# Layer norm of the first half's tokens: normalized and turned on VectorE in the second half's key stage, kept turned in DRAM, and read back for the feed-forward

## The chip, the cores and the metric

The kernel runs on one core of one Trainium2 chip. The metric is the device time of one execution in microseconds (us). The times of the kernel before are the median of three runs and one profiled execution, from which every trace line here is taken.

## What is computed

A gated cross-attention block with a feed-forward layer, on 32 sequences of 64 tokens with 512 features, all in float32. The reference, cut to what matters:

```python
x = x + tanh(g_xattn[0]) * xattn(layernorm(x), ctx, mask, bias, Wq, Wk, Wv, Wo)   # 32 heads of 128
x = x + tanh(g_ffn[0]) * ffn(layernorm(x), weight, bias, lora_A, lora_B, starts)

def ffn(x, ...):                     # x: 32 x 64 x 512
    y = einsum('bsd,od->bso', x, weight) + bias
    lo = einsum('bsr,bor->bso', einsum('bsd,brd->bsr', x, A), Bw)   # rank 16, adapter by sequence
    return y + where(use_lora, lo, 0)
```

The change concerns the second layer norm: the tokens that come out of the attention are normalized along their 512 features, and must then stand with the features along the partitions, so that TensorE can multiply them with `weight`.

## The kernel before, in words

The 2048 tokens are worked on in two halves (`p` = 0 and 1), of 1024 tokens each: `NT` = 8 tiles of 128 tokens, or `NCH` = 2 chunks of 512. Each half goes through a key stage (16 units, one for each pair of heads), a value stage (4 groups of 4 units) and the attention proper (queries, scores, softmax, values, output projection). The feed-forward layer for all four chunks comes at the very end, after the attention of the second half. Every float32 matrix is split into a high and a low float32r part, and a product is three matmuls (`mm3`, line 93, its matmul is line 98). The key, value and query products use a scheme of seven block products for eight (`unit`, line 354): px (p1, later p2 on top), py (p6), pv (p7, later p4 on top) and pz (p5, later p3 on top), each in a bank of PSUM (8 banks in all). VectorE adds a product to the destination (line 356), and only then may the later product be accumulated in the same bank. The last two products of a unit (p4 and p3, `end`, line 381) and the store of its keys to DRAM (`kd`, line 720) are carried into the next unit, after its first product.

The order of the instructions on each engine is written out by hand. Side work is written as generators in a list, `streams`, and `beat()` (line 64) advances each of them by one step after each product; `drain()` runs one to its end. What an engine is given is executed in that order; it waits for its operands where they come from another engine or from a DMA. All DMAs but two of the first are issued by SP, in the order in which they are written, and SP waits for the source or the buffer of each.

In the key stage (`stage_a`, line 684) GpSimd prepares the next unit's key weights (`key_blocks`, line 592; its `fetch`, line 259, loads `rawk`), VectorE computes the moments of `x` (`x_stats`, line 620, through the two-buffer pool `rows`, tag `row`, line 54), and later the weights of the first value group (`blocks_v`). Key tiles (`kT`) live in a pool of two buffers. After the key stage, `x_norm` (line 644) normalizes the transposed `x` with rows of means and scales that it loads from DRAM (`ln`, from `lnd`, line 641).

The output of the first half's attention, `acc`, is stored to DRAM as `x1d` (line 1048). Its moments are computed by `acc_stats` (line 674) in the second half's key stage, from unit 3 on, and its scales by `acc_rstd` (line 679), 28 small VectorE operations that join `streams` in the second value group (line 735).

At the end, `oproj2` (line 1035) does the last eight steps of the output projection (12 matmuls each) and calls `beside(t)` (line 1340) after each. For chunk 0, `beside` normalizes a tile (`ffn_norm`, line 1224, from `x1t`, which `x1_load`, line 1175, has loaded back from `x1d`) into `xn`, and two steps later `ffn_tile` (line 1228) turns it by four TensorE transposes (line 137) into a PSUM bank, from which ScalarE makes the high part (line 1234) and VectorE the low part (line 1235) of the feed-forward's operand `fa`. `ffn_chunk(c)` (line 1273) multiplies chunk c: first the low-rank part (`ffn_lora`, 8 matmuls), then four token tiles (`ffn_out`, 14 matmuls each). Between them it normalizes and turns the tiles of chunk c + 1. Chunks 0 and 1 are the first half's tokens, chunks 2 and 3 those of the second half, which never leave SBUF.

Of the kernel before, what the change touches and what calls it, by code (L numbers as in the profile page):

```python
# [9 lines left out]
F32 = mybir.dt.float32  # L10
F32R = mybir.dt.float32r
# [6 lines left out]
P = 128  # L18
D = 512
KT = D // P  # L20
# [23 lines left out]
def flamingo_block(ctx: ExitStack, tc: tile.TileContext, x, xT, ctxT, bias, mask, gx, gf,  # L44
# [30 lines left out]
    ident = const.tile([P, P], F32, name="ident")  # L75
    make_identity(nc, ident)
    x1d = dram.tile([NT * P, D], F32, name="x1d")
    kd = [[dram.tile([P, 2, TP], F32, name=f"kd{p}_{n}") for n in range(NPR)] for p in range(NPH)]
    lnd = [dram.tile([2, NT, P], F32, name=f"lnd{p}") for p in range(NPH)]
    vd = [[dram.tile([P, NT, 512], F32, name=f"vd{p}_{g}") for g in range(2 * NG)] for p in range(NPH)]  # L80
# [331 lines left out]
    def k_tile(g):  # L412
        return kqp.tile([P, 2, TP], F32, tag="kq", name=f"kT{g}")
# [172 lines left out]
    def paced(g, k):  # L586
        for _ in g:
            yield
            for _ in range(k - 1):
                yield  # L590
# [43 lines left out]
    def x_spread(p):  # L634
        mv, y = mvx[p], rx[p]
        m, mt = [st.tile([P, 4, NT], F32, tag=f"m{i}", name=f"m{i}{p}", bufs=1) for i in range(2)]
        for i in range(4):
            nc.vector.tensor_copy(m[:, i], y if i % 2 else mv[:, :, 0])
        nc.vector.transpose(mt.rearrange("p a b -> p (a b)"), m.rearrange("p a b -> p (a b)"))
        for i in range(4):  # L640
            nc.sync.dma_start(out=lnd[p].rearrange("s t (b q) -> b (s t) q", b=4)[i],
                              in_=mt[i * 32:i * 32 + 2 * NT].rearrange("p a b -> p (a b)"))
# [36 lines left out]
    def acc_rstd(p):  # L679
        for c in range(p * NCH, (p + 1) * NCH):  # L680
            yield from ln_rstd(mv2[:, c * 4:(c + 1) * 4, :], f"f{c}", rstd, c, 5)
            yield

    def stage_a(p, first, fc, res, rot, more, enter, blocks):
        xc, plain = first
        f = None
        for n in range(NPR):
            g = p * NPR + n
            if n == 0 and plain:
                sums = sum_blocks(fc, res, f"c{p}", nc.vector, xc)  # L690
                streams.append(sums)
            if n == 0 and not plain:
                drain(blocks)
            if n == (1 if plain else 0):
                streams.append(key_blocks(p, n + 1))
            if n == 3:
                f = [big(f"f{j}", [P, KT, 512], F32, f"xf{p}_{j}") for j in range(2)]
                t7 = big(rot[7], [P, 2, 1024], F32, f"wvr{p}_0a")
                t8 = big(rot[8], [P, 2, 1024], F32, f"wvr{p}_0b")
                fetch_v(p, 0, [t7[:, 0], t7[:, 1], t8[:, 0], t8[:, 1]])  # L700
                if more:
                    streams.append(paced(more, 2))
                xstat = x_stats(p)
                streams.append(xstat)
            if n == 5:
                vsum = [None] + [rwp.tile([P, 1024], F32, tag=f"r{2 + i}", name=f"vs{p}_0_{i}") for i in range(2)] + [None]
                v0 = paced(blocks_v(p, 0, rot, vsum, nc.vector, K_ORDER), 3)
                streams.append(v0)
            if 6 <= n < 6 + KT:
                for j in range(NCH):  # L710
                    nc.sync.dma_start(out=f[j][:, n - 6, :], in_=xT[p * NCH + j, n - 6])
            if n == 10:
                drain(xstat)
                x_spread(p)
            kt = k_tile(g)
            w = wt[("k", g)]

            def store(kt=kt, n=n):
                for i in range(2):
                    nc.sync.dma_start(out=kd[p][n][:, i, :], in_=kt[:, i, :])  # L720
            if n < 2 and plain:
                for j in range(2):
                    plain_half(w, plain, k_dst(kt), f"k{g}", j, plain["ps"] if n == 0 and j == 0 else None)
                store()
            else:
                if n == 2 and plain:
                    drain(sums)
                carry[:] = [unit(w, xc, None, k_dst(kt), f"k{g}", tuple(carry)), store]
        drain(v0)
        xnorm = paced(x_norm(p, f), 2)  # L730
        streams.append(xnorm)
        xq = {}
        for g in range(NG):
            if g == 1 and p:
                streams.append(acc_rstd(p - 1))
            if g == 2:
                drain(xnorm)
                streams.append(mask_stream(p))
                if p == 0:
                    streams.append(adapt)  # L740
            if g == NG - 1:
                t4 = pieces(rwp.tile([P, 1024], F32, tag="r1", name=f"x{p}t4"))
                fetch("q", p * NPR, "r0")
                bias = enter()
                streams.append(turned_blocks(f, [rot[(7 * NG + i) % 9] for i in range(7)], f"x{p}", nc.gpsimd, keep,
                                             t4, xq, bias, enter))
            for t in range(4):
                if t == 1:
                    if g + 1 < NG:
                        raw = [rwp.tile([P, 1024], F32, tag=f"r{i}", name=f"wvr{p}_{g + 1}_{i}") for i in range(4)]  # L750
                        fetch_v(p, g + 1, raw)
                        streams.append(blocks_v(p, g + 1, rot, None, nc.gpsimd, V_ORDER))
                    if g == NG - 2:
                        keep = {}
                        streams.append(turned_sums(f, f"x{p}", nc.gpsimd, keep))
                if t == 2 and g == NG - 1:
                    streams.append(prep("q", p * NPR, nc.gpsimd))
                vt = kqp.tile([P, 4, 512], F32, tag="kq", name=f"vt{p}_{g}_{t}")
                dst = {(i, j): vt[:, i * 2 + j, :] for i in range(2) for j in range(2)}
                after = unit(wt["v", p, g], xc, slice(t * P, (t + 1) * P), dst, f"v{p}_{g}_{t}", tuple(carry))  # L760

                def store(vt=vt, g=g, t=t):
                    for i in range(2):
                        for j in range(2):
                            nc.sync.dma_start(out=vd[p][2 * g + i][:, j * 4 + t, :], in_=vt[:, i * 2 + j, :])
                carry[:] = [after, store]
        enter()
        return xq
# [434 lines left out]
    def ffn_weights(tags):  # L1203
        wf = [big(tags[i], [P, KT, 512], F32R, f"wf{i}") for i in range(2)]
        ffn_w.update(wf=wf, tags=tags)
        ffn_w["xn"] = big(tags[6], [P, 4, D], F32, "xn")
        ar, br, a2 = ffn_w["ar"], ffn_w["br"], ffn_w["a2"]

        b2 = ffn_w["b2"] = [wbp.tile([P, 512], F32R, tag="wb", name=f"b2{i}") for i in range(2)]
        for _ in range(8):  # L1210
            yield
        nc.scalar.copy(b2[0], br)
        nc.scalar.copy(b2[1][64:P, :], br[64:P, :])
        nc.gpsimd.tensor_tensor(b2[1][0:64, :], br[0:64, :], b2[0][0:64, :].bitcast(F32), ALU.subtract)
        yield
        nc.scalar.copy(a2[:, :, 0:NL * R], ar)
        nc.gpsimd.tensor_tensor(a2[:, :, 64:64 + NL * R], ar, a2[:, :, 0:NL * R].bitcast(F32), ALU.subtract)
        yield
        for kt in range(KT):
            split(ffn_w["raw"][:, kt, :], wf[0][:, kt, :], wf[1][:, kt, :], nc.gpsimd)  # L1220
            yield
        streams.append(paced(x1_load(1), 2))
# [5 lines left out]
    def ffn_tile(c, t):  # L1228
        if t == 0:
            act[c] = [big(ffn_w["tags"][2 + 2 * (c % 2) + i], [P, KT, 512], F32R, f"fa{c}_{i}") for i in range(2)]  # L1230
        hi, lo = act[c]
        ps = transposes(ffn_w["xn"][:, t, :], f"f{c}_{t}")
        h = hi[:, :, t * P:(t + 1) * P]
        nc.scalar.copy(h, ps)
        nc.vector.tensor_tensor(lo[:, :, t * P:(t + 1) * P], ps, h.bitcast(F32), ALU.subtract)

    def ffn_lora(c):
        hi, lo = act[c]
# [34 lines left out]
    def ffn_chunk(c, beside=lambda t: None):  # L1273
        more = c + 1 < NPH * NCH
        ffn_lora(c)
        for t in range(4):
            if more:
                ffn_tile(c + 1, t)
                if t < 3:
                    ffn_norm(c + 1, t + 1)  # L1280
            ffn_out(c, t)
            beside(t)
# [4 lines left out]
    for p in range(NPH):  # L1287
# [34 lines left out]
        else:  # L1322
# [16 lines left out]

            def beside(t):  # L1340
                if t < 4:
                    ffn_norm(0, t)
                else:
                    moments(t - 4)
                if 1 < t < 6:
                    ffn_tile(0, t - 2)
                elif t == 6:
                    ffn_norm(1, 0)

            def rest_of(t):  # L1350
                if t == 0:
# [59 lines left out]
```

## Time and profile before

| | |
|---|---|
| median of 3 runs | 1527.27 us (1527.03 to 1527.68) |
| profiled execution, its own time | 1527.01 us |
| its span, first to last instruction | 1525.2 us |
| TensorE (PE) busy | 1518.5 us, 100% of the span |
| VectorE (DVE), ScalarE (ACT), GpSimd (POOL) busy | 62%, 47%, 69% |
| granted TensorE clock | 1.000 |
| second half's key stage, value stage | about 732 to 881 us, 881 to 1033 us |
| last eight projection steps and feed-forward | about 1433 to 1522 us |

A row of a group of instructions names the line, the engine, the operation, the tile written and the tiles read, the shapes and the number of instructions; after the first bar the busy time and the mean of one in ns, after the second the idle time of the engine just before them and what ended most of it. A row in order of time begins with the start and the length in us, and ends with the idle time before it in brackets. PEld is TensorE's weight load, SPq the queue of DMAs that SP issues. A row on DMA packets gives their number and bytes, and the last figure of a row that begins with q1 is the time that these packets took, as a share of the 16 DMA engines in that stretch.

### The profile page before, as it was taken

The page shows a single profiled execution, that of the slowest core. Times are in us where ns is not written, and L with a number is a line of the kernel's source. Part 1 is how long each engine was busy: PE and PEld are TensorE (multiplying, and loading weights), DVE is VectorE, ACT ScalarE, POOL GpSimd, SP SyncE. Part 2 cuts the span into 40 slices and gives each one's busy share as a digit, 9 for nine tenths or more (in the row PEclk, how much of TensorE's full clock was granted, in tenths as well). Part 3 has the DMA queues.
Part 4 walks back from the last instruction along what each step waited for, and adds up shares of the span by engine and source line. Part 5 has one row for each costly group of instructions (what it writes and reads, how often), then busy time and mean ns, then how long its engine had stood idle before and what let it go on. Part 6 is the DMA issues. An engine that isn't in the chain of part 4 may idle for free.

```text
span 1525.2 us, 25056 instructions
## 1 busy us (share of the span) xinstructions
PE 1518.5 (100%) x8984; PEld 1279.1 (84%) x8984; DVE 941.6 (62%) x1575; ACT 718.4 (47%) x1586; POOL 1048.9 (69%) x1160
## 2 busy tenths in 40 slices
PE   9999999999999999999999999999999999999998
PEld 7888888888888888888888888888888888888887
DVE  5675554376676566666386558437667656666663
ACT  5444233355654664466344423335565466546511
POOL 4999378968675657668789847896867566757310
PEclk9999999999999999999999999999999999999999
DMA  5754544384335263532475454438434426353211
GB/s 207 276 194 152 196 170 168 138 303 157 128 139 180 85 233 126 178 116 95 166 261 194 152 200 166 167 139 312 159 117 143 176 97 222 126 186 113 69 42 69
DMA packets 111071, 248.51 MB, mean 163 GB/s; under 512 B 10241, under 2 KB 44033, under 8 KB 106850
## 3 DMA queue, kind: packets, MB, share of 16 engines
q1 hardware_dynamic: 110658, 246.38, 46.0%
q8 instruction: 71, 1.16, 0.3%
q10 hardware_dynamic: 288, 0.52, 0.1%
q14 instruction: 54, 0.44, 0.1%
HBM read 173.45 MB, written 73.42 MB: 162 GB/s over the span
## 4 chain that ended last, share of the span: by engine, by line
PE 98%; DVE 1%; issue 0%; ACT 0%; POOL 0%; DVEq 0%; POOLq 0%; ACTq 0%
PE pa L98 23%; PE po L982 8%; PE pzv L98 6%; PE pvv L98 6%; PE pxv L98 6%; PE pvq L98 6%; PE pzq L98 6%; PE pxq L98 5%; PE pzk L98 5%; PE pvk L98 5%; PE pxk L98 5%; PE ps L838 4%; PE pyv L98 3%; PE pyq L98 3%; PE pyk L98 3%; PE pf L98 2%
## 5 line engine op out<-in xcount | busy, mean ns | idle before, releaser
L98 PE MATMUL pa<-wo,ch 128*128 128x512 f32 x896 | 278.5, 392 | 0.0
L873 ACT COPY pt<-tp 32x256 f32<-32x256 f32 x456 | 184.0, 403 | 61.0 <-DVE tp L876 50.5
L98 PEld LDWEIGHTS pa<-wo,ch 128*128 128x128 f32 x896 | 166.5, 188 | 34.7
L98 PE MATMUL pa<-wo,cl 128*128 128x512 f32 x448 | 174.8, 390 | 0.0
L1031 DVE TENSOR_TENSOR acc<-pa,acc 128x512 f32<-128x512 f32 x192 | 129.2, 681 | 53.5 <-PE pa L98 53.5
L791 POOL TENSOR_TENSOR sm<-sm,madd 128x512 f32<-128x512 f32 x60 | 77.0, 1295 | 87.1 <-DMA sm<-bias 87.1
L865 POOL TENSOR_TENSOR sm<-sm,r 128x512 f32<-128x512 f32 x64 | 66.9, 1045 | 74.4 <-DVE r L864 73.2
L982 PEld LDWEIGHTS po<-pt,v 128*128 128x128 f32 x960 | 111.6, 192 | 2.2
L982 PE MATMUL po<-pt,v 128*128 128x128 f32 x960 | 112.5, 275 | 0.0
L843 POOL TENSOR_TENSOR sm<-sm,mx 128x512 f32<-128x512 f32 x64 | 66.9, 1047 | 59.8 <-DVE mx L842 59.8
L987 DVE TENSOR_TENSOR cl<-po,ch 128x512 fp32r<-128x512 f32 x112 | 76.5, 690 | 46.1 <-ACT ch L986 45.5
L356 DVE TENSOR_TENSOR vt<-pvv,vt 128x512 f32<-128x512 f32 x64 | 44.0, 688 | 92.7 <-PE pvv L98 92.7
L98 PEld LDWEIGHTS pa<-wo,cl 128*128 128x128 f32 x448 | 84.1, 188 | 18.5 <-DVE cl L987 0.9
L90 POOL TENSOR_TENSOR wo<-rawo,wo 128x512 fp32r<-128x512 f32 x60 | 76.1, 1292 | 22.9 <-ACT wo L89 22.9
L356 DVE TENSOR_TENSOR qT<-pvq,qT 128x512 f32<-128x512 f32 x64 | 44.1, 689 | 73.6 <-PE pvq L98 73.6
L986 ACT CAST ch<-po 128x512 fp32r<-128x512 f32 x112 | 65.6, 589 | 50.1 <-PE po L982 48.1
L356 DVE TENSOR_TENSOR kT<-pvk,kT 128x512 f32<-128x512 f32 x60 | 41.3, 688 | 73.1 <-PE pvk L98 72.8
L378 ACT COPY vt<-pxv 128x512 f32<-128x512 f32 x32 | 18.8, 588 | 131.0 <-PE pxv L98 131.0
L852 ACT ACTIVATE sm<-sm 128x512 f32<-128x512 f32 x60 | 38.0, 633 | 79.0 <-POOL sm L843 75.8
L356 DVE TENSOR_TENSOR qT<-pzq,qT 128x512 f32<-128x512 f32 x64 | 44.2, 691 | 38.1 <-PE pzq L98 37.4
L192 POOL TENSOR_TENSOR vs<-wvr,wvr 128x512 f32<-128x512 f32 x24 | 31.2, 1313 | 48.6 <-DMA wvr<-wv 28.7
L838 PEld LDWEIGHTS ps<-kB,qT 128*64 128x64 f32 x2048 | 61.2, 138 | 3.6 <-issue 1.4
(1001 smaller groups left out, 3908.6 us busy)
## 6 DMA issues: line engine op xcount, KB each, us to landing
kd<-kT SPq DMA_DIRECT2D x64, 512.0 KB, 3.9
vd<-vt SPq DMA_DIRECT2D x128, 256.0 KB, 2.3
kB<-kd SPq DMA_DIRECT2D x32, 1024.0 KB, 9.9
v<-vd SPq DMA_DIRECT2D x32, 1024.0 KB, 7.5
rawq<-wq SPq DMA_DIRECT2D x32, 512.0 KB, 3.3
sm<-bias SPq DMA_DIRECT2D x64, 256.0 KB, 4.3
rawo<-wo SPq DMA_DIRECT2D x32, 512.0 KB, 3.5
rawk<-wk SPq DMA_DIRECT2D x31, 512.0 KB, 5.4
```

The costliest lines, as they stand in the source:

```text
L90: eng.tensor_tensor(lo, raw, hi.bitcast(F32), ALU.subtract)
L98: nc.tensor.matmul(ps, a, b, start=start and i == 0, stop=stop and i == 3 * n - 1, skip_group_check=True)
L356: nc.vector.tensor_tensor(o, ps, i, ALU.add)
L791: nc.gpsimd.tensor_tensor(t, t, masks[p][0], ALU.add)
L838: nc.tensor.matmul(ps[h * S:(h + 1) * S, t, :], qT[:, i, tok], kT[:, i, tok], start=True, stop=True)
L843: nc.gpsimd.tensor_tensor(s, s, mx.unsqueeze(2).to_broadcast([P, NT, S]), ALU.subtract)
L865: nc.gpsimd.tensor_tensor(t, t, r.unsqueeze(2).to_broadcast([P, NT, S]), ALU.mult)
L873: f(pts[n == NPR - 2][dst, i, :, src], of[src, :, ki * 32:(ki + 1) * 32])
L982: nc.tensor.matmul(ps[:, t * P:(t + 1) * P], b["v", n][:, c * 4 + t, i * P:(i + 1) * P], pts[n == NPR - 2][:, i, c * 4 + t, :], start=True ...
L986: nc.scalar.copy(h[:, i, sl], ps)
L987: nc.vector.tensor_tensor(lo[:, i, sl], ps, h[:, i, sl].bitcast(F32), ALU.subtract)
L1031: nc.vector.tensor_tensor(acc[t], ps, acc[t], ALU.add)
```

## The change

The first half's tokens no longer wait for the end. In the second half's key stage, once their moments are there (the rest of `acc_stats` is drained in unit 6), `acc_rstd` follows at once. From unit 11 on a new generator, `acc_turned`, takes the eight tiles one after the other: it loads a tile from `x1d` into a `row` buffer, normalizes it in place on VectorE three steps later, turns it on VectorE into a second `row` buffer (`nc.vector.transpose` turns each block of 32 x 32 by itself), and one step later stores it by four DMAs to a new DRAM tensor `xtd` (512 features x 1024 tokens), each of which takes 32 partitions and puts their 16 blocks where they belong: 512 pieces of 128 bytes. One tile takes four steps. It is drained before the value stage goes on.

At the end, `ffn_load(c)` loads a chunk of `xtd` (four DMAs of 128 x 512), and `ffn_given(c, kt)` only splits a quarter of it into the high and the low part. For chunks 0 and 1 this takes the place of `ffn_norm` and `ffn_tile`. Chunks 2 and 3 are as before. Chunk 0 is loaded where `ffn_weights` begins, chunk 1 after the fourth of the last projection steps, into the same buffer.

```diff
--- before.py
+++ after.py
@@ -75,6 +75,7 @@
     ident = const.tile([P, P], F32, name="ident")
     make_identity(nc, ident)
     x1d = dram.tile([NT * P, D], F32, name="x1d")
+    xtd = dram.tile([D, TP], F32, name="xtd")
     kd = [[dram.tile([P, 2, TP], F32, name=f"kd{p}_{n}") for n in range(NPR)] for p in range(NPH)]
     lnd = [dram.tile([2, NT, P], F32, name=f"lnd{p}") for p in range(NPH)]
     vd = [[dram.tile([P, NT, 512], F32, name=f"vd{p}_{g}") for g in range(2 * NG)] for p in range(NPH)]
@@ -681,6 +682,23 @@
             yield from ln_rstd(mv2[:, c * 4:(c + 1) * 4, :], f"f{c}", rstd, c, 5)
             yield
 
+
+    def acc_turned(p):
+        for t in range(NT):
+            c = p * NCH + t // 4
+            xt = rows.tile([P, D], F32, tag="row", name=f"xr{p}_{t}")
+            nc.sync.dma_start(out=xt, in_=x1d[t * P:(t + 1) * P, :])
+            for _ in range(3):
+                yield
+            ln_apply(xt, xt, mv2[:, c * 4:(c + 1) * 4, :], rstd[c], t % 4)
+            tp = rows.tile([P, D], F32, tag="row", name=f"xq{p}_{t}")
+            nc.vector.transpose(tp, xt)
+            yield
+            for i in range(4):
+                nc.sync.dma_start(
+                    out=xtd.rearrange("(a b) t -> b a t", b=32)[:, :, t * P + i * 32:t * P + (i + 1) * 32],
+                    in_=tp[i * 32:(i + 1) * 32].rearrange("p (a b) -> p a b", b=32))
+
     def stage_a(p, first, fc, res, rot, more, enter, blocks):
         xc, plain = first
         f = None
@@ -699,7 +717,8 @@
                 t8 = big(rot[8], [P, 2, 1024], F32, f"wvr{p}_0b")
                 fetch_v(p, 0, [t7[:, 0], t7[:, 1], t8[:, 0], t8[:, 1]])
                 if more:
-                    streams.append(paced(more, 2))
+                    more = paced(more, 2)
+                    streams.append(more)
                 xstat = x_stats(p)
                 streams.append(xstat)
             if n == 5:
@@ -709,9 +728,15 @@
             if 6 <= n < 6 + KT:
                 for j in range(NCH):
                     nc.sync.dma_start(out=f[j][:, n - 6, :], in_=xT[p * NCH + j, n - 6])
+            if n == 6 and p:
+                drain(more)
+                streams.append(acc_rstd(p - 1))
             if n == 10:
                 drain(xstat)
                 x_spread(p)
+            if n == 11 and p:
+                turned_acc = acc_turned(p - 1)
+                streams.append(turned_acc)
             kt = k_tile(g)
             w = wt[("k", g)]
 
@@ -727,12 +752,12 @@
                     drain(sums)
                 carry[:] = [unit(w, xc, None, k_dst(kt), f"k{g}", tuple(carry)), store]
         drain(v0)
+        if p:
+            drain(turned_acc)
         xnorm = paced(x_norm(p, f), 2)
         streams.append(xnorm)
         xq = {}
         for g in range(NG):
-            if g == 1 and p:
-                streams.append(acc_rstd(p - 1))
             if g == 2:
                 drain(xnorm)
                 streams.append(mask_stream(p))
@@ -1203,7 +1228,7 @@
     def ffn_weights(tags):
         wf = [big(tags[i], [P, KT, 512], F32R, f"wf{i}") for i in range(2)]
         ffn_w.update(wf=wf, tags=tags)
-        ffn_w["xn"] = big(tags[6], [P, 4, D], F32, "xn")
+        ffn_load(0)
         ar, br, a2 = ffn_w["ar"], ffn_w["br"], ffn_w["a2"]
 
         b2 = ffn_w["b2"] = [wbp.tile([P, 512], F32R, tag="wb", name=f"b2{i}") for i in range(2)]
@@ -1233,6 +1258,17 @@
         h = hi[:, :, t * P:(t + 1) * P]
         nc.scalar.copy(h, ps)
         nc.vector.tensor_tensor(lo[:, :, t * P:(t + 1) * P], ps, h.bitcast(F32), ALU.subtract)
+
+
+    def ffn_load(c):
+        ffn_w["xt"] = big(ffn_w["tags"][6], [P, KT, 512], F32, f"xt{c}")
+        for kt in range(KT):
+            nc.sync.dma_start(out=ffn_w["xt"][:, kt, :], in_=xtd[kt * P:(kt + 1) * P, c * 512:(c + 1) * 512])
+
+    def ffn_given(c, kt):
+        if kt == 0:
+            act[c] = [big(ffn_w["tags"][2 + 2 * (c % 2) + i], [P, KT, 512], F32R, f"fa{c}_{i}") for i in range(2)]
+        split(ffn_w["xt"][:, kt, :], act[c][0][:, kt, :], act[c][1][:, kt, :], nc.vector)
 
     def ffn_lora(c):
         hi, lo = act[c]
@@ -1274,7 +1310,12 @@
         more = c + 1 < NPH * NCH
         ffn_lora(c)
         for t in range(4):
-            if more:
+            if c + 1 < NCH:
+                for kt in range(KT)[2 * t:2 * t + 2]:
+                    ffn_given(c + 1, kt)
+                if t == 1:
+                    ffn_w["xn"] = big(ffn_w["tags"][6], [P, 4, D], F32, "xn")
+            elif more:
                 ffn_tile(c + 1, t)
                 if t < 3:
                     ffn_norm(c + 1, t + 1)
@@ -1339,13 +1380,11 @@
 
             def beside(t):
                 if t < 4:
-                    ffn_norm(0, t)
+                    ffn_given(0, t)
                 else:
                     moments(t - 4)
-                if 1 < t < 6:
-                    ffn_tile(0, t - 2)
-                elif t == 6:
-                    ffn_norm(1, 0)
+                if t == 3:
+                    ffn_load(1)
 
             def rest_of(t):
                 if t == 0:
```

## The prediction, made before the changed kernel was run

> **What bounds the kernel now.** I read the busy table first, then the chain of work that ended last, then the end of the run in order of time, then the stage into which the work is moved.
>
> ```profile
> PE 1518.5 (100%) x8984; PEld 1279.1 (84%) x8984; DVE 941.6 (62%) x1575; ACT 718.4 (47%) x1586; POOL 1048.9 (69%) x1160
> ...
> PE 98%; DVE 1%; issue 0%; ACT 0%; POOL 0%; DVEq 0%; POOLq 0%; ACTq 0%
> ```
>
> TensorE is the path for 98% of the span. So an instruction taken from TensorE is worth its own length, and anything else costs nothing until it makes TensorE wait. What is removed stands in these rows (groups by line in the last 100 us):
>
> ```profile
> L1235 DVE TENSOR_TENSOR fa<-tpf,fa 128x512 fp32r<-128x512 f32 x16 | 10.9, 682 | 3.0 <-ACT fa L1234 3.0
> ...
> L137 PE MATMUL tpf<-ident,xn 128*128 128x128 f32 x64 | 9.8, 275 | 0.3 <-DVE xn L132 0.2
> ...
> L1234 ACT CAST fa<-tpf 128x512 fp32r<-128x512 f32 x16 | 9.3, 584 | 40.2 <-PE tpf L137 40.2
> ```
>
> Matmuls overlap, so their 275 ns are not their price. The price is read from the rhythm of the projection's last steps, from one accumulation to the next (12 matmuls with, then without, four transposes between):
>
> ```profile
> 1447.53 0.69 DVE L1046 TENSOR_TENSOR acc<-pa,acc 128x512 f32<-128x512 f32 x1 [1.45 <-PE pa L98]
> ...
> 1450.74 0.69 DVE L1046 TENSOR_TENSOR acc<-pa,acc 128x512 f32<-128x512 f32 x1 [1.13 <-PE pa L98]
> ...
> 1456.65 0.69 DVE L1046 TENSOR_TENSOR acc<-pa,acc 128x512 f32<-128x512 f32 x1 [0.78 <-PE pa L98]
> ```
>
> 3.21 us with transposes; the step to 1453.93 still has them, the one to 1456.65 has none and takes 2.72. Four transposes cost 0.48 us. The new work goes into the second half's key stage. There the chain is TensorE alone, 1.36 us for a product of six matmuls, seven products (9.52 us) a unit, and SP issues three large transfers a unit (start, length, queue, line, transfer):
>
> ```profile
> 838.61 0.80 SPq L720 DMA_DIRECT2D kd<-kT  x2
> 839.49 0.74 SPq L264 DMA_DIRECT2D rawk<-wk  x1
> ...
> DMA packets 432, 1.57 MB, mean 183 GB/s; under 512 B 48, under 2 KB 48, under 8 KB 432
> ...
> q1 hardware_dynamic: 432, 1.57, 50.7%
> ```
>
> The last two lines are the DMA view of 839.4 to 848: 1.5 MB of payload keeps 16 engines 50.7% busy for 8.6 us, 4.3 us of ring time in a unit. In 825 to 850 VectorE is 59% busy. It has time, but works in order, and each wait for a DMA holds the PSUM reads behind it.
>
> **What the Trainium skill says.** "DMA: Bandwidth & Descriptors", section "Queues, rings and completion order": one issuing engine has one ring on each DMA engine, consumed in ring order. So a load issued behind stores waits for them. No run here shows it directly. Same page, "Specifications": full rate needs 512 B or more; smaller is read-modify-write. This trace has one store of 128-byte pieces, `lnd` (line 641), four issues in 826 to 829.2:
>
> ```profile
> DMA packets 128, 0.01 MB, mean 3 GB/s; under 512 B 128, under 2 KB 128, under 8 KB 128
> ...
> q1 hardware_dynamic: 128, 0.01, 2.4%
> ...
> DMA packets 1040, 1.05 MB, mean 140 GB/s; under 512 B 16, under 2 KB 1040, under 8 KB 1040
> ...
> q1 hardware_dynamic: 1040, 1.05, 42.8%
> ```
>
> 2.4% of 16 engines for 3.2 us is 1.23 us for 128 packets, 9.6 ns each; half are completions, so data packets lie between 9.6 and 19 ns, in an idle ring. No penalty shows, but nothing was saturated. The last pair (1400 to 1407.5, a `v` load) gives 50 ns at 1 KB; `out` stores give 88 at 2 KB. That line meets 128 B near 17 ns. Same page, "Alternative transpose paths": VectorE turns 32 x 32 blocks only. It agrees with the code, which places the blocks by four DMAs. The 128x512 transpose of line 876 takes 0.695 us in 62 runs.
>
> **The change, part by part.**
>
> *Removed from TensorE.* 32 transposes, eight groups of four. Four sit in the projection's last steps: 4 x 0.48 = 1.92. Four sit in feed-forward chunk 0, which takes 16.86 us (1456.45 to 1473.31); without transposes a chunk is 8 x 0.227 + 4 x 3.17 = 14.50, so 2.36, small waits for `xn` included. **Gain 4.28 us, all on the path.**
>
> *Added in the tail.* Eight splits from SBUF (ScalarE copy, VectorE subtract) replace eight from PSUM and eight `xn` (0.54 us): no more work. `xt0` is four loads issued near 1408, behind `v`; its first use is after 1437. `xt1` is issued near 1447 and used at 1459; a 256 KB `x1t` load lands in 2.6 to 7.7. Both at 0, hidden by the projection; without that cover, one landing. The next weight load `rawo` passes behind `xt0` on SP, but its slot frees only at 1424.8: 0.
>
> *Moved scalars.* 28 small operations (about 0.25 us, 7 us in all) go from value to key stage, beside units 6 to 10. VectorE is 72% busy in 800 to 825, so it stays below 90%: 0, at most 1. Draining the remaining statistics moves nothing in the order.
>
> *Added in the key stage.* Per tile: load 256 KB, normalize 0.54, turn 0.70, four stores of 512 pieces of 128 B, and then on the same SP queue the next load. VectorE meets a tile every four products, 5.44 us. The tiles form a loop, since two `row` buffers serve both uses: transpose t, its four issues, load t+1, transpose t+1. One turn: 0.1 handover, four issues, 2.6 (shortest landing of a 256 KB load) and 1.24 on VectorE. An issue of three dimensions is not bounded tightly: `lnd` 0.41, `v` 0.52, `la` (512 pieces, too) 0.65. I take 0.52: **6.0 us**, against 5.44 available. Ends: 5.6 and 6.5.
>
> Ring time is on top where large transfers lie ahead. The stores are 2048 packets, at 17 ns over 16 engines 2.2 us. Tile 0 is turned by 841.8 (today's additions of `kT27` plus 1.24). `kd` and `rawk` of 838.6 hold the rings until 838.6 + 1.3 (first byte, as in the `v` load) + 4.3 = 844.2; stores to 846.4, load 0.7, receipt 0.6, 1.24: 848.9, a turn of 7.1. The same collision meets tiles 2 and 4 (7.2 each); tile 5 sees `kd` alone. Seven turns: 7.1 + 2 x 7.2 + 4 x 6.0 = 45.5, so tile 7 is turned at 887.3.
>
> What that costs: TensorE may add product `p4` of a unit only after VectorE has read `p7`. Behind tile 7 stands that read for unit 31, due when `p4` starts, at 882.7 today (after 873.17, seven products): tile 7 must be done by 882.0. The loss is 887.3 - 882.0 = **5.3 us**. On SP, `kd` stores and `rawk` loads stand behind stores that wait for a transpose; ScalarE's casts and GpSimd's subtractions of key weights wait for them. Raw weights land in 5.4 and are read about 0.7 us later, though TensorE wants them some 6 us after that. I add 0.5. Loads of `ln` and `wvr` queue behind the last stores: TensorE is late by as much, 0. The stage's cost is 5.8.
>
> *Sum.* The profiled execution took 1527.01 (span 1525.2 and 1.8 around it): 1527.01 - 4.28 + 5.8 = 1528.5. The median of runs is 0.26 above: **1528.8**.
>
> **Rivals.** *The loop fits.* With issues of 0.41 and 9.6 ns packets, turns are 5.6, and 6.1 to 6.2 at collisions: 40.9 us, tile 7 at 882.7, loss 0.7 or none. For it: VectorE waits only 1.4 us for eight `xs` loads now, at a ring share of 0.77. Against it: those loads were issued without waiting for stores. Time 1523.0 to 1523.7: faster.
>
> *The rings fill.* In the key stage, small stores occupy the rings longer than a unit has room. A unit has 1.75 tiles: 1.75 x (128 packets x price + 0.7) + 4.3 reaches 9.52 us at 18 ns. Past about 19 ns turns grow beyond 6.3 (7.5 at collisions), the loss beyond 7.3 and the kernel is slower. If a 128-byte store costs what 512 B would on my line, 31 ns, stores take 4.0 and a turn 7.9: 14 to 20 us lost, 1537 to 1543; I name 1540. For it: the skill's warning and the thin margin. Against it: the `lnd` packets.
>
> *The gain isn't there* (another wait fills the 4.28, as the chunk's VectorE work might) and the stage is free: 1527.3. The removed groups are back to back on TensorE, which speaks against it.
>
> **How the numbers follow.** The loop sets the pace, 1524.2 to 1533: 0.34, likeliest at 1528.8, which is its own range too. It fits, 1522.9 to 1524.2: 0.34. Rings fill, 1533 to 1555 and from 1530.3 on at its mild end: 0.28. Gain lost: 0.04. A measurement here tells 0.2%, 3.05 us, from no change. Faster is the second case, 0.34. Same is 0.27 of the first and the last, 0.31. Slower is 0.07 of the first and the third, 0.35. The range is 1522.9 to 1541: left out are the far part of the full rings (about 0.1) and a larger gain (0.05).
>
> **What would show it.** Right: no `tpf` with `x1t`, chunk 0 near 14.6 us; VectorE waits for `xr` loads or `xtd` stores, turns near 6 to 7 us, TensorE gaps before `pvk`, `pzk` products in 850 to 890. The first rival: turns 5.44 apart, no gaps. The second: ring share 0.9 or more and stores landing late. Wrong altogether: gaps in the value stage or the tail.

## The result, and the profile after

| | before | after |
|---|---|---|
| median | 1527.22 us (1527.03 to 1527.68, 8 runs) | 1531.66 us (1530.65 to 1532.07, 8 runs) |
| ratio after to before | | 1.0027 (1.0018 to 1.0037) |
| profiled execution, its own time (span) | 1527.01 us (1525.2) | 1530.93 us (1529.2) |

The change makes the kernel slower by 4.44 us by the medians, 0.27% by the ratio over all runs. The profiled execution lies 0.73 below the median of its runs; it is 3.92 above that of before.

The page of the kernel after, busy times and the chain of work that ended last:

```profile
PE 1517.8 (99%) x8952; PEld 1276.9 (84%) x8952; DVE 943.8 (62%) x1583; ACT 717.9 (47%) x1586; POOL 1049.4 (69%) x1160
...
PE 95%; DVE 2%; DMA 1%; SPq 1%; issue 0%; POOL 0%; ACT 0%; DVEq 0%; POOLq 0%; ACTq 0%
```

TensorE executes 32 instructions fewer, the transposes, and yet the span is longer. The second line says where to look: the path was TensorE for 98% of the span, now for 95%, and VectorE, DMA and SP's queue have come onto it. A share of 1% is 15 us; something that is neither long nor frequent has become the path for some 50 us. So the next view is the chain, cut to the key stage (840 to 892). Each row is a start, a length, and what was on the chain:

```profile
by line: DMA xr<-x1d 43.9%; SPq L698 24.9%; DVE xr L133 11.3%; DVE xq L695 11.1%; issue 3.8%; PE pvk L99 3.1%; DVE kT L357 2.5%; DVE wv_0p L189 1.1%; DVEq L133 0.0%
...
864.72 3.04 DMA xr<-x1d
867.76 0.03 issue
867.78 0.56 DVE xr L133
868.34 0.02 issue
868.36 0.72 DVE xq L695
869.09 0.02 issue
869.10 0.32 SPq L698
869.42 0.05 issue
869.47 0.48 SPq L698
...
871.17 4.15 DMA xr<-x1d
...
889.16 0.71 DVE xq L695
889.87 0.59 DVE kT L357
890.46 0.14 issue
890.60 1.63 PE pvk L99 x6
```

From 841 to 890 the path does not touch TensorE once. It is the loop: the load of a tile (3.04), normalize (0.56), transpose (0.72), the four stores issued by SP, the next load (4.15), and so on through eight tiles. A *turn* below is one round of this loop, from the end of one tile's transpose to the end of the next; seven turns lie between the first tile and the last. The end shows how it reaches TensorE: after the last transpose (889.87) VectorE reads p7 of unit 31 (`kT`, 0.59), and only then does p4 start, at 890.60. Before, it started at 882.53:

```profile
882.53 1.52 PE L98 MATMUL pvk<-c1p,wk31p 128*128 128x512 f32 x6
```

The waits of the kernel after in 840 to 895 (total us, times, longest):

```profile
DVE xr L133 <- DMA xr<-x1d: 19.9, 7, 4.3
...
PE pvk L99 <- DVE kT L357: 3.7, 2, 2.7
...
PE pzk L99 <- DVE kT L357: 0.8, 1, 0.8
```

VectorE stands still seven times for a load, 19.9 us in all. TensorE then shows three gaps of only 4.5 us, though it is 8.1 late at the end. The starts of its products tell the rest: each should follow the one before by 1.36 us, and what exceeds that sums to 8.0 between 852 and 892. Of it 5.3 lie at these three waits (0.9, 3.2 and 1.2: a group's drawn end runs past the start of the next, so a gap looks shorter than it is), 1.7 at two products that ran at a lower clock (last section), and 1.0 at others, half of it where key weights came late.

In the tail, the projection's steps and feed-forward chunk 0 of the kernel after, in order of time:

```profile
1446.37 0.62 PE L99 MATMUL pa<-wo,ch 128*128 128x512 f32 x2
...
1449.09 0.62 PE L99 MATMUL pa<-wo,ch 128*128 128x512 f32 x2
...
1462.69 0.39 PE L1278 MATMUL pt<-fa,a 128*128 128x512 f32 x1
...
1477.20 0.39 PE L1278 MATMUL pt<-fa,a 128*128 128x512 f32 x1
```

The last two rows are the starts of chunk 0 and of chunk 1. Before, they were:

```profile
1456.45 0.39 PE L1242 MATMUL pt<-fa,a 128*128 128x512 f32 x1
...
1473.31 0.39 PE L1242 MATMUL pt<-fa,a 128*128 128x512 f32 x1
```

All projection steps take 2.72 us now, and chunk 0 takes 14.51 (16.86 before). It starts 6.24 later than before, and the four groups of transposes saved ahead of it are worth 1.92: the key stage made the kernel 8.2 us late in this execution. 8.2 - 1.92 - 2.35 is the 3.9 that the profiled times differ by.

### The profile page after: what moved, and what is told of

Same layout as the page of the kernel before. It is cut to its first block, busy times and chain, and to the rows that moved or that the text cites. A ratio compares the mean times of both kernels' runs of the same rounds, so it can differ in the third digit from the quotient of the medians.

```text
span 1529.2 us, 25072 instructions
## 1 busy us (share of the span) xinstructions
PE 1517.8 (99%) x8952; PEld 1276.9 (84%) x8952; DVE 943.8 (62%) x1583; ACT 717.9 (47%) x1586; POOL 1049.4 (69%) x1160
## 4 chain that ended last, share of the span: by engine, by line
PE 95%; DVE 2%; DMA 1%; SPq 1%; issue 0%; POOL 0%; ACT 0%; DVEq 0%; POOLq 0%; ACTq 0%
PE pa L99 23%; PE po L1007 7%; PE pzv L99 6%; PE pvv L99 6%; PE pxv L99 6%; PE pvq L99 6%; PE pzq L99 6%; PE pxq L99 5%; PE pvk L99 5%; PE pzk L99 5%; PE pxk L99 5%; PE ps L863 4%; PE pyv L99 3%; PE pyq L99 3%; PE pf L99 3%; PE pyk L99 2%
## 5 line engine op out<-in xcount | busy, mean ns | idle before, releaser
L357 DVE TENSOR_TENSOR vt<-pzv,vt 128x512 f32<-128x512 f32 x64 | 44.2, 690 | 33.1 <-PE pzv L99 32.4
```

Source lines behind the costliest of these rows:

```text
L357: nc.vector.tensor_tensor(o, ps, i, ALU.add)
```

## The experiments

The change has two halves, a gain in the tail and a cost in the key stage, which add up to a small number. So each run's *stage cost* is given: its distance to the kernel before on the same chip, plus the tail's gain of 4.59 that `tail_only` measured. By it the changed kernel costs 4.44 + 4.59 = 9.0. The intervals of the ratios reach 1.3 to 2.4 us to either side, so the times alone do not tell apart stage costs that lie closer than some 2 us. My theory: the loop sets the pace, so what shortens a turn or gives it more time takes the cost away. Rivals: the DMA engines are full; the gain is not there. The texts of what was expected call the theory and the first rival loop theory and ring theory.

**The tail alone, and the key stage alone.** `tail_only`:

```diff
-            if n == 11 and p:
-                turned_acc = acc_turned(p - 1)
-                streams.append(turned_acc)
...
-        if p:
-            drain(turned_acc)
...
-            nc.sync.dma_start(out=ffn_w["xt"][:, kt, :], in_=xtd[kt * P:(kt + 1) * P, c * 512:(c + 1) * 512])
+            nc.sync.dma_start(out=ffn_w["xt"][:, kt, :], in_=x1d[(c * 4 + kt) * P:(c * 4 + kt + 1) * P, :])
```

> The tail of the change without its key-stage work: nothing is normalized or turned in the key stage, and the feed-forward loads of the first half read the unnormalized rows of x1d in the same shape. So the normalizing and turning of these tokens are left out. It prices the gain by itself. Theory: the 4.28 us of the prediction, so 1522.9 (1522.5 to 1523.3). Rival: the tail's own loads and splits take part of it back, 1524 to 1526.

Measured 1523.09 (1522.95 to 1523.6, 6 runs) against 1527.68 on that chip, ratio 0.997 (0.9959 to 0.9982): 4.59 us faster. The gain is there in full, and the moved scalars, which this kernel keeps, cost nothing that can be seen. The rival that it is not there falls.

`old_tail` is the opposite, the key stage's work with the feed-forward as before:

```diff
-        ffn_load(0)
+        ffn_w["xn"] = big(tags[6], [P, 4, D], F32, "xn")
...
-            if c + 1 < NCH:
-                for kt in range(KT)[2 * t:2 * t + 2]:
-                    ffn_given(c + 1, kt)
-                if t == 1:
-                    ffn_w["xn"] = big(ffn_w["tags"][6], [P, 4, D], F32, "xn")
-            elif more:
+            if more:
...
-                    ffn_given(0, t)
+                    ffn_norm(0, t)
```

> The key-stage work of the change with the tail of the kernel before: tiles are turned and stored, but the feed-forward normalizes and transposes as before and nobody reads what was stored. If loss and gain add up: 1531.66 + 4.28 = 1535.9, that is 8 to 8.7 us over the kernel before. If the tail of the change costs something by itself in the presence of the key stage's lateness, less: 1533 to 1534.

Measured 1536.16 (1535.34 to 1536.73, 4 runs) against 1527.22, ratio 1.0059 (1.0043 to 1.0074): 8.9 slower. The stage alone costs 8.9, and 8.9 - 4.6 gives the change within 0.2. The halves add, as far as the runs can tell; nothing hides between them.

**One arm of the loop taken away.** `no_load` normalizes tiles that already lie in SBUF:

```diff
-            nc.sync.dma_start(out=xt, in_=x1d[t * P:(t + 1) * P, :])
...
-            ln_apply(xt, xt, mv2[:, c * 4:(c + 1) * 4, :], rstd[c], t % 4)
+            ln_apply(xt, f[t // 4][:, t % 4, :], mv2[:, c * 4:(c + 1) * 4, :], rstd[c], t % 4)
```

> The tiles of the key stage are not loaded from x1d: VectorE normalizes data that lie in SBUF anyway (the transposed x) into the row buffer, turns them and stores them as in the change. So the right tokens are left out; issues of stores, their packets and all VectorE operations stay. Loop theory (VectorE waits for the load at the end of a chain of issues): what is left of the turn is 2.05 of issues, 1.9 of landing and 0.8 of handover and transpose, 4.8 us against 5.44, so the loss falls from 8 to 0 to 2, which is 1523 to 1525. Ring theory (the small stores fill the rings): they are all still there, so at least 1527.

Measured 1523.2 (1523.0 to 1523.97, 7 runs) against 1527.22, ratio 0.9974 (0.9964 to 0.9985): stage cost 0.6. All the stores, with all their small packets, are still there. VectorE's main wait for a DMA is now this one:

```profile
DVE xq L694 <- DMA xtd<-xq: 4.9, 4, 2.0
```

That is a buffer waiting for its stores, and it does not reach TensorE. So what costs is the load inside the loop, and not VectorE's work or the stores. The bytes of the eight loads (2.1 MB) are gone too; that it is not these is shown by `every_five` below, which has them all.

**One arm doubled.** `eight_stores` stores each tile twice, the second time to a tensor that nobody reads:

```diff
-            for i in range(4):
-                nc.sync.dma_start(
-                    out=xtd.rearrange("(a b) t -> b a t", b=32)[:, :, t * P + i * 32:t * P + (i + 1) * 32],
-                    in_=tp[i * 32:(i + 1) * 32].rearrange("p (a b) -> p a b", b=32))
+            for dst in (xtd, xt2):
+                for i in range(4):
+                    nc.sync.dma_start(
+                        out=dst.rearrange("(a b) t -> b a t", b=32)[:, :, t * P + i * 32:t * P + (i + 1) * 32],
+                        in_=tp[i * 32:(i + 1) * 32].rearrange("p (a b) -> p a b", b=32))
```

> Each of the four stores of a tile is issued twice, the second time to a DRAM tensor that nobody reads. Loop theory: each turn grows by four issues, 2.0 us, so that the seven turns take 47.6 + 14 = 62 us, the last tile is turned at 904 and the loss is 22 us against the tail alone: 1545 (1542 to 1549). If the issues don't matter and only the packets' time does (10 ns each by the DMA views of the change and of big_pieces, 1.3 us a tile), less than half of that: 1537 to 1541.

Measured 1547.91 (1547.34 to 1549.21, 4 runs) against 1527.22, ratio 1.0136 (1.0122 to 1.0149): stage cost 25.3, as the loop has it and not as the packets alone would (2.2 of it is a lower clock, last section). SP's queue and VectorE in it, in order of time:

```profile
842.38 2.02 SPq L700 DMA_DIRECT2D xtd<-xq  x4
844.44 2.32 SPq L700 DMA_DIRECT2D xt<-xq  x4
846.81 0.51 SPq L691 DMA_DIRECT2D xr<-x1d  x1
```

```profile
849.75 0.83 DVE L134 TENSOR_SCALAR xr<-xr,mv,yf 128x512 f32<-128x512 f32 x1 [4.90 <-DMA xr<-x1d]
```

The load is issued 2.32 later. From its issue to the normalize it takes 2.94 here, and 2.87 to 3.29 in all seven turns, against 2.76 to 4.18 in the changed kernel. Twice the small packets did not lengthen the load's way; twice the issues put it off, one for one.

**The same bytes in large pieces.** `big_pieces` stores each tile in 2 KB pieces, without placing the blocks:

```diff
+            flat = xtd.rearrange("a b -> (a b)")
             for i in range(4):
-                nc.sync.dma_start(
-                    out=xtd.rearrange("(a b) t -> b a t", b=32)[:, :, t * P + i * 32:t * P + (i + 1) * 32],
-                    in_=tp[i * 32:(i + 1) * 32].rearrange("p (a b) -> p a b", b=32))
+                k = (t * 4 + i) * 32 * D
+                nc.sync.dma_start(out=flat[k:k + 32 * D].rearrange("(p e) -> p e", e=D), in_=tp[i * 32:(i + 1) * 32])
```

> The four stores of a tile write 2 KB pieces, unplaced, instead of 128-byte pieces: the same issues, bytes, buffers and waits, but 128 packets a tile instead of 2048. The kernel leaves out the placing of the 32 x 32 blocks, so that the feed-forward of the first half reads mixed features. Ring theory: the loss of 8 us is in the small packets, so it goes: at most 1524.5. Loop theory: most of the turn is the issues, the landing and VectorE, and only what the load waits behind the stores' packets goes, 0 to 0.7 us a turn: loss 4 to 7, 1527 to 1530.5.

Measured 1528.95 (1527.38 to 1530.15, 12 runs) against 1527.68, ratio 1.0009 (1.0001 to 1.0018): stage cost 5.9. The DMA view of 842 to 890, first of the changed kernel, then of this one:

```profile
DMA packets 17384, 9.47 MB, mean 197 GB/s; under 512 B 15077, under 2 KB 15077, under 8 KB 17382
...
q1 hardware_dynamic: 17382, 9.44, 70.2%
```

```profile
DMA packets 4229, 9.96 MB, mean 208 GB/s; under 512 B 816, under 2 KB 816, under 8 KB 4226
...
q1 hardware_dynamic: 4226, 9.92, 63.9%
```

13155 packets fewer, and the share falls only from 70.2 to 63.9%. In engine time (share x 48 x 16) that is 539 against 491 us. There are 14261 small packets fewer and 1106 others more; with these at the 88 ns of the `out` stores, the small ones come to (48 + 97) / 14261 = 10 ns each, an estimate. The packets' own records in the trace of the changed kernel have 16384 pieces of 128 bytes at 12.2 ns on average, where a 2 KB piece takes 84 at the median. The seven turns take 44.0 us, 3.6 fewer: 0.26 a turn from shorter issues (1.79 against 2.06 from the end of the transpose to the next load) and 0.24 from the load's way, from its issue to its use. The profiled execution, from which these are, was one of the two fastest (1527.47; the others but one took 1528.5 to 1530.15, at a granted clock of 0.998 or 0.999 instead of 1.000). So the small pieces are a third of the cost by the medians (3.1 of 9.0) and nearly half by the profiled executions (3.9 of 8.3), half of it through SP.

**The order of load and stores.** `load_first` issues the next load ahead of the four stores:

```diff
             yield
+            if t + 1 < NT:
+                xt = load(t + 1)
             for i in range(4):
```

> The next tile's load is issued ahead of the four stores of the tile just turned. Everything else is as in the change. Loop theory (the turn of the tile loop, 6.4 to 7.6 us against 5.44 available, is the loss): the load no longer waits for four issues (2.05 us), so its side of the turn is 0.5 issue + 2.7 to 3.0 landing + 1.3 on VectorE = 4.5 to 4.8; the other side, the stores that must land before the buffer is turned into again, is 0.5 + 2.05 + 1.9 + 0.7 = 5.2. Both are below 5.44, so the loss falls from 8 us to 0 to 2 and the kernel takes 1523 to 1525. Ring theory (the small stores fill the DMA rings): the same packets pass in the same units, so it stays at 1529 or more.

Measured 1526.33 (1526.0 to 1527.02, 13 runs) against 1527.68, ratio 0.9992 (0.9984 to 1.0001): stage cost 3.2. The direction is right, the size a miss. Its waits in 830 to 912:

```profile
DVE xr L133 <- DMA xr<-x1d: 7.5, 5, 3.1
...
DVE xq L699 <- DMA xtd<-xq: 6.2, 7, 2.1
...
PE pvk L99 <- DVE kT L357: 2.7, 2, 2.1
```

Two things took the place of what was gained. The transpose now waits for the stores of the tile before, seven times: it writes into the buffer from which these are read. In the changed kernel it has to as well, but there the load stands behind them on SP and comes later in any case. And two turns are still 8.66 and 7.58 us, the others 5.1 to 6.1: there a load meets the `kd` stores and the `rawk` load. The DMA view of this kernel in such a place (853.7 to 858.8):

```profile
q1 hardware_dynamic: 1953, 1.39, 104.1%
```

The engines are full for 5 us. (A packet counts whole in the stretch in which it starts, so a share can pass 100%.) The rival of full engines is right for such moments, not for the stage.

`act_load` is `load_first` with the loads issued by ScalarE, to see whether another queue gets past:

```diff
-            nc.sync.dma_start(out=xt, in_=x1d[t * P:(t + 1) * P, :])
+            nc.scalar.dma_start(out=xt, in_=x1d[t * P:(t + 1) * P, :])
```

> As load_first, but the load of the next tile is issued by ScalarE. In load_first two turns were 8.65 and 7.6 us, where the load stood behind 1.5 MB of key stores and weight loads on SP's queue. If loads wait there for their place in SP's queue and its rings, a load from another queue passes them: no turn over 6.5 us, loss 0 to 1.5, 1523 to 1524.6. If the engines' bandwidth is what is short, the load lands no sooner: 1525.5 to 1527. ScalarE's own waits, in order, may eat part of the gain.

Measured 1527.07 (1526.12 to 1528.93, 13 runs) against 1527.22, ratio 0.9998 (0.999 to 1.0007): stage cost 4.4, no better than from SP. Issue and use at the collision, from the views of ScalarE's queue and of VectorE:

```profile
853.62 0.35 ACTq L689 DMA_DIRECT2D xr<-x1d  x1
```

```profile
859.03 0.86 DVE L133 TENSOR_SCALAR xr<-xr,mv,yf 128x512 f32<-128x512 f32 x1 [2.10 <-DMA xr<-x1d]
```

5.41 us from issue to use, and 5.06 from SP in `load_first`. That agrees with the Trainium skill, "DMA: Bandwidth & Descriptors", section "Issuing engines are not separate DMA queues": all issuers share the same 16 engines and interleave on them.

**The pace.** `every_five` leaves the loop as it is and asks for a tile every five products, not four, from one unit earlier:

```diff
-            for _ in range(3):
+            for _ in range(4):
...
-            if n == 11 and p:
+            if n == 10 and p:
```

> A tile every five products instead of four, from unit 10 instead of 11. Loop theory: 6.80 us are available for a turn, against 6.4 to 7.6 (mean 6.8) taken now; the lag at the end is about 0, the loss 0 to 1, and the kernel takes 1523 to 1524.5. Ring theory: 1.4 tiles a unit instead of 1.75, so that the rings are relieved by a fifth of the small stores only: loss 3 to 5, 1526 to 1528.

Measured **1523.36** (1522.83 to 1524.59, 8 runs) against 1527.68, ratio 0.9972 (0.9962 to 0.9982): stage cost 0.3. Its waits in 830 to 912, and its busy times in 842 to 882 (us, then PE, PEld, DVE, ACT, POOL, clock, DMA share, GB/s):

```profile
DVE xr L133 <- DMA xr<-x1d: 9.3, 6, 2.4
```

```profile
842.00:882.00 40.00, 40.00 (x178) 33.11 (x178) 26.75 (x40) 15.38 (x38) 32.02 (x41) 1.00 0.75 214
```

The turns are no shorter (6.45 to 7.49, mean 6.86), but five products give 6.80. VectorE waits 9.3 us and TensorE not at all, at a DMA share of 0.75, above the 0.72 of the changed kernel in the same stretch. A stage that is full cannot run better at a higher share.

`unit_ten` has the earlier start without the slower pace:

```diff
-            if n == 11 and p:
+            if n == 10 and p:
```

> The change begun one unit (9.52 us) earlier, at the pace of the change, a tile every four products. every_five changed the start and the pace; this changes the start alone. Loop theory: the turns stay at 6.4 to 7.6 against 5.44, and the last tile's deadline moves forward with its place in the order: the loss stays at 6 to 9 us, 1529.5 to 1532. Rival (the stage's end is too crowded, room is what helped): the loss is halved or gone, 1523 to 1527.

Measured 1533.12 (1531.65 to 1533.68, 6 runs) against 1527.40, ratio 1.0035 (1.0023 to 1.0047): stage cost 10.3, 1.1 above what I expected at most. So the head start alone does not help; a slower pace without it was not tried. With a tile every four products the reads behind the last tile come due a unit earlier too. Its last tile is turned at 881.48; the deadline of 881.8 (next section, point 3) less 9.52 is 872.3, so it is 9.2 late. After the gap that this makes, TensorE's clock fell, which cost 1.7 us on top (last section); without that, the time would lie in the range.

`five_load_first` joins `every_five` and `load_first`:

```diff
+            if t + 1 < NT:
+                xt = load(t + 1)
...
-            for _ in range(3):
+            for _ in range(4):
...
-            if n == 11 and p:
+            if n == 10 and p:
```

> every_five with the next load ahead of the stores. Loop theory: every_five has no loss left to remove (0.3 us over the tail alone, within its spread), so this is the same: 1523.0 to 1523.6. If the waits of VectorE for loads (9.3 us in every_five) still cost TensorE something, 0.3 to 1 us less than every_five.

Measured **1522.93** (1522.79 to 1523.71, 7 runs) against 1527.40, ratio 0.9972 (0.9961 to 0.9982): stage cost 0.1. VectorE waits 1.8 us in all. `every_five` and this one are the two best; both keep the tail's gain, and the runs do not tell them apart. A third `row` buffer, which would let a load go further ahead, was not tried.

## Why the prediction came out as it did

The forecast was 1528.8 in a range of 1522.9 to 1541.0; the time is 1531.66. The mechanism of the likeliest case, the loop, was the right one, and the size of its cost was too small. The sign was left open: the likeliest time stood at +0.1%, with 0.34 for faster, 0.31 for the same and 0.35 for slower. That the time lies inside a range of 18 us says little; the single terms say more.

1. *The gain: right.* 4.28 predicted; 1.92 and 2.35 in the trace; 4.59 by `tail_only`. Tail loads, splits and moved scalars at 0 held.
2. *The loop as the bound, through p7's read: right.* The chain shows it step by step, `no_load`, `eight_stores` and `every_five` move it as they should.
3. *The deadline: right but for 0.2.* The prediction counted from 873.17, where the chain view lets the product begin, after the drawn end of the one before. In order of time it starts at 873.01, so p4 of unit 31 is due at 882.53 and the last tile, 0.73 before that (889.87 to 890.60), at 881.8, not 882.0. It is turned at 889.87, 8.1 late, and p4 is 8.1 late. In the other kernels of the same start, lateness and the stage cost of the same, profiled execution stay together: 3.9 and 3.7 (`load_first`), 4.3 and 4.7 (`act_load`), 4.6 and 4.4 (`big_pieces`), 23.1 and 25.5 (`eight_stores`).
4. *The turn: too short.* This is the term that was mis-sized. "Seven turns 45.5, tile 7 turned at 887.3" became 47.6 and 889.87:

| us | predicted | measured |
|---|---|---|
| first tile turned | 841.8 | 842.24 |
| transpose to load, handover and four issues, seven turns | 15.3 | 14.5 |
| load to normalize, collisions included | 21.6 | 23.1 |
| normalize and transpose | 8.7 | 10.1 |
| last tile turned | 887.3 | 889.87 |

The landing was taken as "2.6 (shortest landing of a 256 KB load)". Here a load needs 2.76 to 4.18 from issue to use, and even `big_pieces`, without small packets, 2.77 to 3.40. The shortest of a wide spread was the wrong value for a term that is repeated seven times in a loaded stage. That is 1.5 of the miss. Nearly as much, 1.4, is VectorE: the normalize was taken at 0.54, and beside GpSimd it takes 0.83 to 1.0 (last section). The issues, taken at 0.52 each, were slightly overpriced, which gave 0.8 back.

5. *Packets: overpriced.* 17 ns were taken. The estimate from two kernels is 10, the packets' own records have 12.2, within the 9.6 to 19 that `lnd` had shown. At 12.2 ns a piece of 128 bytes moves 10 bytes per ns, at 84 ns one of 2 KB moves 24. So small pieces do stay below the full rate, as the Trainium skill has it for those under 512 B ("DMA: Bandwidth & Descriptors", section "Specifications"); but a price beyond that, such as the rival's 31 ns, does not show. The two errors, packets too dear and landings too short, went against each other, and the second was larger.
6. *Collisions: two of three.* Turns with tiles 2 and 4 were to take 7.2 and take 7.11 and 7.57. The first took 6.64, not 7.1. The plain turns are 6.4 to 6.7, not 6.0.
7. *The 0.5 for the weights.* In the trace the stage costs 8.2 with the last tile 8.1 late, so 0.1 is left for everything else. Key weights did hold TensorE for about 0.5 at two products (871.8 and 873.6), but it had to wait for the next tile anyway.

Together: 5.8 + 0.4 (start) + 2.1 (turns) + 0.2 (deadline) - 0.4 (weights) = 8.1 in the trace, where 8.2 was lost. The median of runs stands 0.7 above the profiled one, which no step explains.

Rivals: that the loop fits was wrong for four products and true for five. That the rings fill was wrong as the stage's limit (share 0.70, and 0.75 without loss) and true for 5 us at a collision.

## What to carry to other kernels

When side work is a loop through a DMA (load, compute, store, with the next load behind the stores on the same queue), work out its turn with typical landings of the loaded stage, not the best, and compare it with the pace at which an engine in order will meet it: here a turn took 6.8 us on average where 5.44 were given, and seven such turns put the main engine 8.1 us behind. A slower pace that starts earlier is then worth more than a faster loop (stage cost 0.3 against 3.2), and an earlier start without a slower pace was worth nothing (10.3). Where a change is a gain and a cost in two places, run each half alone: two numbers of 4.6 and 9.0 say more than their difference of 4.4.

## What was not expected of the hardware

**The clock after a short gap.** TensorE's gap of 2.71 us ahead of unit 30's p4 in the changed kernel, the product after it, and the windows behind it (columns as above):

```profile
878.16 2.66 PE L99 MATMUL pvk<-c1p,wk30p 128*128 128x512 f32 x6 [2.71 <-DVE kT L357]
880.62 2.12 PE L99 MATMUL pzk<-c1p,wk30p 128*128 128x512 f32 x6
```

```profile
874.00:878.00 4.00, 1.45 (x6) 0.67 (x4) 2.51 (x4) 1.09 (x3) 3.84 (x7) 1.00 0.88 330
878.00:880.00 2.00, 1.84 (x5) 1.52 (x6) 0.70 (x2) 1.51 (x5) 2.00 (x4) 0.61 0.67 114
880.00:882.00 2.00, 2.00 (x6) 1.54 (x6) 0.47 (x1) 0.49 (x2) 2.00 (x4) 0.54 0.36 120
882.00:884.00 2.00, 2.00 (x11) 1.61 (x10) 1.86 (x4) 0.00 (x0) 0.98 (x2) 1.00 0.00 0
```

In these two stretches the mean clock is 0.61 and 0.54, and six matmuls take 2.66 and then 2.12 instead of some 1.6. The clock records behind these means have one period of exactly half clock, from 878.43 to 881.84. In all kernels, but for their very start and end, such periods are 3.41 us long, or twice that (`eight_stores`), and the times between them are multiples of 3.41 too (873.81 is 256 of them), so the clock changes only at the edges of windows that run on regardless of the work. Laid over these windows, the rows of TensorE show what decides: from full clock, half clock followed each window in which TensorE stood idle for 1.98 us or more (1.98 to 2.75, seven windows, in the changed kernel, `old_tail`, `unit_ten` and `eight_stores`), and none in which it stood idle for 1.63 or less (`big_pieces`). So about half a window is enough, and the gap's length alone does not decide: one of 2.24 us in `unit_ten` (1.62 for the six matmuls after it) and one of 2.06 in `load_first` fell across an edge, with at most 1.54 on one side, and cost no clock. The idle times are as drawn, with ends that are modelled. The Trainium skill, "TensorE: Matmul & The Clock Gate", section "What's actually happening", has half clock after an idle window of about 3.4 us; the length of the window agrees, but it need not be idle throughout.

From start to start the two products of the changed kernel above took 2.46 and 1.96 instead of 1.36, 1.7 us in all. This costs nothing that can be seen there, since TensorE still waits for the last tile afterwards (1.03 us at 890.60). In `unit_ten` no wait comes afterwards, and it does cost. The first row is of before, the others of `unit_ten`:

```profile
873.01 1.52 PE L98 MATMUL pvk<-c1p,wk30p 128*128 128x512 f32 x6
```

```profile
882.21 2.56 PE L99 MATMUL pvk<-c1p,wk30p 128*128 128x512 f32 x6 [2.75 <-DVE kT L357]
884.57 2.22 PE L99 MATMUL pzk<-c1p,wk30p 128*128 128x512 f32 x6
...
893.46 1.52 PE L99 MATMUL pvk<-c1p,wk31p 128*128 128x512 f32 x6
```

TensorE is 9.2 us late at 882.21 and 10.9 late at 893.46 (882.53 before), with no wait between: 1.7 us for the clock. In `eight_stores` it is 23.1 late at the last p4 and 25.3 late two products on.

**VectorE beside GpSimd.** The same normalize of 128x512 takes 0.55 us where GpSimd stands still (867 and 888 in the changed kernel) and 0.83 to 1.00 where a GpSimd addition has begun just before it (840, 847, 854 and 881). In each of these four it ends 0.27 to 0.29 us after that addition ends, as it does wherever it is lengthened in the other runs, so it seems to wait for it; the two rows of 854:

```profile
853.84 0.73 POOL L300 TENSOR_TENSOR wk29p<-wsk,wk29p 128x256 fp32r<-128x256 f32 x1 [0.22 <-ACT wk29p L296]
```

```profile
854.01 0.83 DVE L133 TENSOR_SCALAR xr<-xr,mv,yf 128x512 f32<-128x512 f32 x1 [1.70 <-DMA xr<-x1d]
```

Where it begins near the end of one (861 and 875) it takes 0.55, and GpSimd's next addition takes 1.00 and 0.84 instead of 0.74. It agrees with the Trainium skill, "SBUF — State Buffer", section "SBUF: two separate sides", by which the two share a port pair that one instruction holds to its end. The transpose, at 0.71 in all of them, shows nothing of it.
